# Strassen's form for one more step of the last batch pair, its transposes moved off TensorE, one input loaded earlier and one later, with a new order of work

## The chip, the cores and the metric

The kernel runs on one core of one Trainium2 chip. The metric is the device time of one execution in microseconds (us), taken as the median of several runs. A core has engines that each run their own instruction stream in order and meet through semaphores: TensorE (PE) with its matmuls and weight loads, VectorE (DVE), ScalarE (ACT), GpSimd (POOL), and SyncE (SP), which here issues most of the DMA transfers. PE writes its sums to PSUM banks, from which VectorE and ScalarE read them.

## The reference

Sixteen batches of 1024 nodes with 128 features go through two graph layers that share one symmetric 0/1 matrix `adj` (1024 x 1024). Cut to what is computed:

```python
# layer 0: attention over adj
h = x @ others_weight
u1, u2 = h @ a1, h @ a2
e = u1[:, idx1] + u2[:, idx2]            # pair indices: gathers from u1 and u2
e = jnp.where(e >= 0, e, ALPHA * e)
att = softmax(jnp.where(adj > 0, e, NEG_BIG), axis=1)
x = layernorm(x + att @ h + x @ self_weight)

# layer 1: five gated steps, in_matrix = out_matrix = adj
for step in range(5):
    m = adj @ h                          # m_in = m_out
    av = concat([m, m])
    u3 = h @ u3_w.T + u3_b
    z = sigmoid(av @ w3_w.T + w3_b + u3)
    r = sigmoid(av @ w4_w.T + w4_b + u3)
    hv = tanh(av @ w5_w.T + w5_b + (r * h) @ u5_w.T + u5_b)
    h = (1 - z) * h + z * hv
x = layernorm(x + h)
```

## The kernel before

**Pairs, steps and halves.** The batches run in eight pairs, q = 0 to 7, pair q holding batches 2q and 2q+1. For each pair there are layer 0 of its two batches and then the steps s = 0 to 4 of layer 1. Within a batch, h is kept transposed (features on the 128 partitions, nodes along the free side) in the tile hT and worked on in two halves of 512 nodes. The odd batch is kept with its sign flipped, and the signs of the activations are turned to fit.

**One step.** `messages` makes m = adj @ h. Its left operand are blocks of h with nodes on the partitions, each split by `split` into a high part (ACT cast, L661) and the rest (VectorE subtraction, L665), so that two fast matmuls carry the accuracy of one float32 matmul; `product` (L669 to L673) is eight such matmuls of 128x128 by 128x512. There are two forms. The plain form (pairs and steps in `PLAIN`) makes four products for each batch: 8 for the pair. The other is Strassen's, in Winograd's variant: the two batches side by side are cut into 2x2 blocks, and 7 products are made of the blocks x11, x12, x22 and of sums s1 to s4 that VectorE adds up first (`add_to`, L1127), with tables of adj's blocks as the right operand. ACT copies the results out (L1185, L1187) and VectorE combines them (L1195); the plain form has four ACT copies (L1158).

`gates` (from L1269) then makes, for each batch and half: the u3 product (L1301), a copy of it by ACT into the bank of the z gate (gz, L1304), the matmuls of r and z onto them (L1311), the tanh of each (L1314), r times h (L1321), the two matmuls of v (L1327, L1328), tanh (L1336), and three VectorE operations that give the new h (L1339, L1342, L1345).

**Turning h for the next step.** The blocks need nodes on the partitions, hT has features there. There are two ways. On PE (pairs and steps in `TURNED`, also some outputs; `on_pe`, L316): four 128x128 transposes for each half (`transposes`, L617 to L623), from which `split` reads in PSUM. Otherwise: VectorE transposes within 32x32 squares (`turn`, L631, tile T), `away` writes the squares to DRAM at swapped places with four 64 KB DMAs from SP (L641, X), and `back` reads 256 KB back (L649, tile G). The next step's splits and sums read G.

**Layer 0.** For each batch: x is loaded as xt (L703, L706), h and the two scores come from PE (L715), the scores are turned and sent to DRAM as ud (L760); pb reads one row of them back on all partitions (L767) and uu gathers 4-byte elements (L775). VectorE sums with adj and pb (junk, L854), and q (L843) and rz (L873 to L877) give the scales by which ACT (L906) and VectorE (L912) make the blocks blk for the products po (L673). For batches 4 to 7 the product of x with self_weight is made far ahead, in the first 40 us (`ahead`, from L474): x goes into tiles of the r and z pools (named r_x and z_x), the result (m_px) to DRAM as PX (L491), and it comes back when the batch's turn is there. For batch 7 that load waits until batch 1's gather uu is issued, as do the later weights (L383) and the xt loads of batches from 4 on.

**The order of work.** Every operation is given to a list scheduler, `Plan`, with its engine, an estimated length and a rank. A rank is 10 for each pair, 4.2 for each step, an offset for the kind of operation (the table `D`) and a correction for single batches, steps and halves (the table `NUDGE`). The scheduler plays the run through with these lengths and at each point lets an engine start the ready operation of lowest rank. What it finds is the order of each engine's instructions; on the chip each engine goes through its list in order. So a changed rank or length anywhere can move instructions elsewhere.

After all batches but the last ones are far, a flag that tells whether an exact second path is needed is read by every engine (L1789; the flag is written by VectorE, L1576); for SP this read stands in the middle of its stream of DMA issues.

Of the kernel before, what the change touches and what calls it, by code (L numbers as in the profile page):

```python
# [17 lines left out]
P = 128  # L18
N = 1024
HALF = 512  # L20
# [7 lines left out]
MOST = math.exp(HIGH - SHIFT)  # L28
TINY = 1e-30
LARGE = 0.999e30  # L30
PLAIN = {(0, 0), (0, 1), (0, 2), (7, 2), (7, 3), (7, 4)}
LATER = 0.75
AHEAD = range(4, 8)
LATE = 3001
TURNED = {(0, 0), (7, 2), (7, 3)}
IDLE = 44
NUDGE = {(3, 2): 1.8, (3, 3): 1.55, (0, 1): 0.15, (1, 1): 1.05, (2, 3): -1.05, (3, 1): -1.35, (3, 0): -0.15, (0, 2): 1.0, (2, 2): 1.25, (1, 4): 0.6, (1, 3): -2.85, (0, 3): -0.15, (1, 2): -0.15, (4, 0): 0.55, (2, 0): 2.25, (2, 1): 0.05, (4, 4): -1.7, (2, 4): 0.3, (7, 3): 1.1, (5, 4): -2.25, (4, 3): 0.8, (6, 3): 0.45, (6, 4): -0.05, (8, 2): 1.35, 10: 0.05, (11, 3): -0.9, (11, 4): 1.55, (7, 2): 1.0, (8, 3): -1.15, (12, 3): -0.45, (13, 3): 0.0, (12, 0): 1.6, (10, 3): -0.35, (8, 4): -0.55, (12, 4): -1.45, (12, 1): -0.95, (11, 2): -1.05, 12: 0.35, (13, 4): 2.7, (13, 0): 1.35, (11, 1): 1.1, (12, 2): -2.15, (10, 4): -1.1, (15, 0): -0.6, (14, 2): -0.6, (1, 0): -1.3, 3: -0.05, (0, 0): -0.3, (0, 4): 0.9, 4: -1.35, (4, 2): 0.05, (5, 1): -4.25, (3, 4): -0.25, 7: 0.75, (5, 3): 1.5, (6, 1): -0.25, (8, 1): 0.0, (9, 3): -4.85, 8: -1.65, (9, 2): -0.5, 11: 0.15, (7, 4): 1.2, 14: 0.1, (9, 1): 2.35, (15, 1): -0.5, (10, 2): 1.15, (14, 0): -0.45, (14, 3): 1.3, (11, 0): -0.2, (15, 4): 1.15, (15, 3): 1.2, 0: 0.85, (4, 1): -0.15, 6: -1.05, (7, 0): 0.35, (6, 2): -0.8, (5, 2): -0.6, (8, 0): 0.35, (6, 0): -0.05, (14, 4): -0.2, (14, 1): 0.3, 2: -0.35, (5, 0): 0.6, (7, 1): -0.35, (9, 0): -0.4, (9, 4): 0.9, 9: -0.15, (10, 0): 1.15, (10, 1): 0.0, 13: 0.15, (13, 2): -0.3, (15, 4, 0): 0.3, (15, 2): 0.3, ('add', 14, 1): 0.15, ('add', 15, 0): -0.1, ('ln', 14, 1): -0.5, ('ln', 15, 0): -1.2, 15: -0.05, ('add', 14, 0): -0.6, 1: 0.6, 5: 0.05, (13, 1): 0.15, ('ln', 15, 1): -0.05, ('old', 15): -0.05, ('add', 15, 1): 0.3}


class Plan:  # L40
# [106 lines left out]
def kernel(  # L147
# [51 lines left out]
    nc = tc.nc  # L199
# [27 lines left out]
    def exact(pools):  # L227
# [7 lines left out]
        tab = table.tile([P, 4, NC // 2, HALF], F32R, tag="tab", name="tab")  # L235
# [40 lines left out]
        def T(t, dtype=None, shape=None):  # L276
            if t not in tiles:
                _, sh, dt, _ = kinds[t[0]]
                tiles[t] = places[t[0]].tile(
                    shape or sh, dtype or dt, tag=t[0], name="_".join(map(str, t)).replace("-", "n")  # L280
                )
            return tiles[t]
# [25 lines left out]
        def sp(*a, **k):  # L308
            plan.add("SP", *a, **k)


        D = dict(m=0.45, pu=-0.1, u=3.45, pr=0.75, pz=0.85, r=1.45, pv=0.25, z=2.8, hv=0.5, h=-0.8, tr=1.85, o=6.35, ln=2.5, out=4.4, l1=-10.7, l2=-9, l3=-2.4, l4=-3.5, l5=-7.25)
        D.update(l6=-1.35, l7=-0.5, l8=-4.4, q=10, s=4.2, even=1, base=-1.0, q1=-3, b1=4.3, lz=-4.5, l1_0=-5.5, l2_0=-4, lz_0=-4.2, l3_0=-2, l4_0=-4.5, l5_0=-9, l6_0=-2.5, l7_0=-5, l8_0=-3.5)
        D.update(l1_1=-12, l2_1=-8, lz_1=-3, l3_1=-2.2, l4_1=-5, l5_1=-9.5, l6_1=-2.3, l7_1=-1.8, l8_1=-2, tab=8, tabc=1.5, cl=-5.4, ca=-50.5, cr=-51, px=-4.0, own=-2, ownw=-3.4)

        def on_pe(b, what):  # L316

# [33 lines left out]
        def early_loads():  # L351
# [14 lines left out]
            writes=[(boot, "early"), (ws, "early"), (x0, "early"), (("xt", 1), "early"), *((t, "early") for t in staged)],  # L366
# [13 lines left out]
        def late_loads():  # L380

            def load(t, what, to, by):
                sp(450, -7.9, lambda: nc.sync.dma_start(to(), by), reads=[(("b1",), 0)], writes=[(t, what)], lag=2600)  # L383

            for j, w in enumerate((w3_t, w4_t, w5_t)):
                load(
                    boot,
                    ("late", j),
                    lambda j=j: W("w345")[:, 256 * j : 256 * (j + 1)].rearrange("p (t e) -> p t e", t=2),
                    w.rearrange("(t p) e -> p t e", p=P),  # L390
                )
            load(("uw",), 0, lambda: u3, u3_t)
            load(("uw",), 1, lambda: u5, u5_t)
            for j, v in enumerate((w3_b, w4_b, w5_b, u3_b, u5_b)):
                load(ws, ("b", j), lambda j=j: T(ws)[j : j + 1, 3 * P : 4 * P], v.rearrange("(o p) -> o p", o=1))
# [78 lines left out]
        def ahead():  # L474
            for b in AHEAD:
                d = ("PX", b)
                for e in range(2):
                    bank, px, x = ("ps", "ahead", b, e), ("m", "px", b, e), ("rz"[e], "x", b)
                    hs = slice(e * HALF, (e + 1) * HALF)
                    sp(450, -91, lambda x=x, b=b, hs=hs: nc.sync.dma_start(T(x), x_t[b][:, hs]), reads=[(("b1",), 0)] if b == AHEAD[-1] else [], writes=[(x, "sent")], lag=0)  # L480
                    plan.add("DMA", 4 * 190, -102.7, lambda: None, reads=[(x, "sent")], writes=[(x, 0)])

                    def px_(bank=bank, x=x):
                        nc.tensor.matmul(T(bank), wsi, T(x), start=True, stop=True)

                    pe(F, 8000, px_, reads=[(x, 0), (("wsi",), 0)], writes=[(bank, 0)])
                    act(A, D["px"], lambda bank=bank, px=px: nc.scalar.copy(T(px), T(bank)), reads=[(bank, 0)], writes=[(px, 0)])
                    sp(
                        450,
                        -20,  # L490
                        lambda d=d, px=px, hs=hs: nc.sync.dma_start(T(d)[:, hs], T(px)),  # L491
                        reads=[(px, 0)],
                        writes=[(d, e)],
                    )
# [188 lines left out]
        def layer0(b):  # L683

            first = rank0(b) - (60 if b == 0 else 0)

            def lv(k):
                return D.get(f"{k}_{b}", D[k])

            rank = first + lv("l1")  # L690
            xt, hx, pb, u, us, uu, ud = (
                ("xt", b), ("hx", b), ("pb", b), ("u3", b), ("us", b), ("uu", b), ("ud", b)
            )
# [3 lines left out]
            if b in (2, 3):  # L697
                xt = ("hT", "x", b)
            junk = ("junk", b)
            q, zs, rz, hT = ("q", b), ("zs", b), ("rz", b), ("hT", b)  # L700
            yT, y0, yd = ([(k, b, g) for g in range(2)] for k in ("yT", "y0", "yd"))
            if b in (2, 3):
                sp(450, -90, lambda: nc.sync.dma_start(T(xt), x_t[b]), writes=[(xt, "sent")], lag=0)  # L703
                plan.add("DMA", 8 * 190, -102.5, lambda: None, reads=[(xt, "sent")], writes=[(xt, 0), (xt, 1)])
            elif b >= 2:
                sp(450, rank, lambda: nc.sync.dma_start(T(xt), x_t[b]), reads=[(("b1",), 0)], writes=[(xt, 0), (xt, 1)], lag=3500)  # L706

            for g in range(4):
                ph = ("ps", "g", b, "ph", g)
# [38 lines left out]
            if b >= 1:  # L748
# [5 lines left out]
                    reads=[(u, 0), (u, 1)],  # L754
                    writes=[(us, 0)],
# [5 lines left out]
                    reads=[(us, 0)],  # L761
                    writes=[(ud, 0)],
# [5 lines left out]
                    reads=[(ud, 0)],  # L768
                    writes=[(pb, 0), (pb, 1)],
                    lag=3000,  # L770
# [3 lines left out]
                    for w in range(2):  # L774
                        nc.sync.dma_start(T(uu)[:, w, :], T(ud)[w + 1].rearrange("(c p two) -> two p c", p=P, two=2)[w])  # L775

                sp(950, rank, uu_, reads=[(ud, 0)], writes=[(uu, 0), *([(("b1",), 0)] if b == 1 else [])], lag=3000)

            else:

                if True:

                    for e in range(2):
                        pp = ("ps", "p", b, e)
                        hs = slice(e * HALF, (e + 1) * HALF)
# [42 lines left out]
            rank = first + lv("l2")  # L828
# [21 lines left out]
            rank = rank0(b) + lv("lz")  # L850
# [17 lines left out]
            for k in range(2 if b == 0 else 1):  # L868
# [10 lines left out]
                def least_():  # L879
# [9 lines left out]
                    reads=[(q, 0), *((zs, c) for c in ks), *((("A",), c, 1) for c in ks)],  # L889
                    writes=[(rz, k)] if b == 0 else [(rz, 0), (rz, 1)],  # L890
# [5 lines left out]
            rank = rank0(b) + lv("l3")  # L896
            size = 1 if b == 0 else 4
            hl = [[("blk", b, w, g) for g in range(2)] for w in range(2)]
            for w in range(2):
                for c0 in range(0, NC, size):  # L900
# [20 lines left out]
                    r = [*((hx, g) for g in sorted({c // 2 for c in cs})), (rz, c0 // 4)]  # L921
# [3 lines left out]
            rank = rank0(b) + lv("l4")  # L925
            left = slice(0, HALF)
            right = slice(HALF, N)
            for g in range(2):
# [6 lines left out]
                for c0 in range(0, 4, size):  # L935
                    cs = range(c0, c0 + size)

                    def po_(g=g, po=po, cs=cs):
# [6 lines left out]
                        reads=[(k, 4 * g + c, j) for k, j in ((hl[0][g], 0), (hl[0][g], 1), (("A",), 0)) for c in cs],  # L945
                        writes=[(po, 0)],
# [7 lines left out]
            px = ("xt", b, "px") if b in AHEAD else ("gz", b, "px") if b == 0 else ("ps", "acc", b, "px")  # L954
            if b in AHEAD:
# [5 lines left out]
                    reads=[(d, 0), (d, 1), (hx, 3)],  # L961
                    writes=[(px, 0)],
                    lag=2800,
                )
            else:
# [4 lines left out]
                    reads=[(xt, 0), (("wsi",), 0), *([(yT[1], "p")] if b else [])],  # L970
                    writes=[(px, 0)],
# [5 lines left out]
                reads=[(px, 0), (yT[0], "s")],  # L977
                writes=[(yT[0], 0)],
# [61 lines left out]
            for g in range(2):  # L1040
# [5 lines left out]
                def h(g=g):  # L1046
# [9 lines left out]
                    lag=4000,  # L1056
# [783 lines left out]
```

## Time and profile before

| | us |
|---|---|
| median of 3 runs (1446.03 to 1447.8) | 1446.27 |
| the profiled execution's own time | 1445.98 |
| its span | 1444.2 |
| PE busy | 1429.6 (99%) |
| VectorE busy | 1158.9 (80%) |
| ScalarE busy | 891.8 (62%) |
| GpSimd busy | 198.0 (14%) |

The profile is of one execution of the program. The span runs from the first to the last instruction; the execution's own time is 1.8 us more. A busy time is the sum of the instructions of an engine. The chain that ended last is found from the last instruction back, at each step to what released it, so its shares say which engine set the end. A wait is given as engine, line and tile that waited, what released it, the total, the number of times and the longest. In the views by group or in time a row reads: line, engine, operation, out <- in, shapes, and in brackets the idle time just before and what ended it. The granted clock of TensorE was 0.998 of full speed on the mean.

### The profile page before, as it was taken

To read this page: it belongs to the slowest core of one execution; us is meant where nothing else is said; L and a number is where in the kernel's file an instruction comes from. 1 tells how busy PE (TensorE), PEld (TensorE's weight loads), DVE (VectorE), ACT (ScalarE), POOL (GpSimd) and SP (SyncE) were. 2 spreads that over 40 slices of the span, in tenths; PEclk is the share of its full clock that TensorE was granted. 3 is DMA by queue.
4 is the path that set the end of the run, shared out by engine and by line. 5 is a ranking of instruction groups with operands and counts; after the bars stand their busy time and mean duration, and the time that the engine had idled before them with its cause. 6 is when DMAs were issued, how large, how long until landed. Compare 5 with 4: busy or idle time off the path is not lost.

```text
span 1444.2 us, 17589 instructions
## 1 busy us (share of the span) xinstructions
PE 1429.6 (99%) x4955; PEld 897.0 (62%) x4955; DVE 1158.9 (80%) x2756; ACT 891.8 (62%) x1789; POOL 198.0 (14%) x324
## 2 busy tenths in 40 slices
PE   9999999999999999999999999999999999999997
PEld 7676666566666666566666665565656665556664
DVE  6897987998888988689888898677889876775635
ACT  5665665756666666567576667666666565654544
POOL 1121001003001021011110112010300212000202
PEclk9999999999999999999999999999999999999999
DMA  8334445534455544264444634444333544323111
GB/s 277 114 116 137 145 134 158 154 108 144 112 139 164 152 136 135 52 183 125 139 127 115 172 106 137 126 131 119 92 97 104 144 148 109 83 57 96 38 42 32
DMA packets 193458, 176.84 MB, mean 122 GB/s; under 512 B 37442, under 2 KB 142152, under 8 KB 193352
## 3 DMA queue, kind: packets, MB, share of 16 engines
q1 hardware_dynamic: 187046, 157.41, 39.2%
q0 software_dynamic: 5888, 17.83, 3.8%
q8 instruction: 41, 0.67, 0.2%
q14 instruction: 65, 0.53, 0.1%
q10 hardware_dynamic: 418, 0.39, 0.1%
HBM read 97.19 MB, written 78.36 MB: 122 GB/s over the span
## 4 chain that ended last, share of the span: by engine, by line
PE 97%; DVE 1%; DMA 1%; ACT 1%; issue 0%; SPq 0%; POOL 0%; POOLq 0%; DVEq 0%; ACTq 0%
PE ps_acc_a L673 17%; PE ps_g_r L1311 10%; PE gz L1311 9%; PE ps_g_v L1327 9%; PE ps_g_v L1328 9%; PE ps_g_r L1301 9%; PE ps_acc_c L673 9%; PE ps_acc_po L673 8%; PE ps_acc L673 6%; PE gz L673 4%; PE ps_g_ph L715 2%; PE ps_acc_po L983 1%; PE ps_acc_px L969 1%; PE ps_idle L449 1%; PE ps_t L623 1%; DMA uu<-ud 1%
## 5 line engine op out<-in xcount | busy, mean ns | idle before, releaser
L1339 DVE TENSOR_TENSOR hv<-hv,hT 128x512 f32<-128x512 f32 x158 | 108.4, 686 | 85.4 <-ACT hv L1336 84.4
L1327 PE MATMUL ps_g_v<-m,wm 128*128 128x512 f32 x318 | 162.6, 592 | 0.6 <-ACT m L1187 0.6
L1311 PE MATMUL ps_g_r<-m,wm 128*128 128x512 f32 x320 | 161.7, 593 | 0.7 <-ACT gz L1304 0.7
L1328 PE MATMUL ps_g_v<-r,u5h 128*128 128x512 f32 x318 | 162.4, 592 | 0.0
L1311 PE MATMUL gz<-m,wm 128*128 128x512 f32 x320 | 161.0, 592 | 0.0
L673 PE MATMUL ps_acc_a<-tab,blk_s 128*128 128x512 f32 x544 | 159.5, 435 | 0.0
L1301 PE MATMUL ps_g_r<-hT,u 128*128 128x512 f32 x320 | 158.9, 592 | 0.0
L1321 DVE SCALAR_TENSOR_TENSOR r<-r,hT 128x512 f32<-128x512 f32 x160 | 109.2, 684 | 60.5 <-ACT r L1314 60.1
L1314 ACT ACTIVATE r<-ps_g_r,bh 128x512 f32<-128x512 f32 x160 | 109.9, 687 | 68.2 <-PE ps_g_r L1311 67.9
L673 PE MATMUL ps_acc_po<-adj,blk 128*128 128x512 f32 x512 | 144.8, 427 | 2.4 <-DVE blk L912 1.4
L673 PEld LDWEIGHTS ps_acc_a<-tab,blk_s 128*128 128x128 f32 x544 | 102.4, 188 | 45.5 <-issue 23.7
L1304 ACT COPY gz<-ps_g_r 128x512 f32<-128x512 f32 x160 | 91.2, 575 | 50.8 <-PE ps_g_r L1301 49.8
L673 PEld LDWEIGHTS ps_acc_po<-adj,blk 128*128 128x128 f32 x512 | 95.7, 188 | 40.6 <-issue 15.6
L1314 ACT ACTIVATE z<-gz,bh 128x512 f32<-128x512 f32 x160 | 109.1, 688 | 18.5 <-PE gz L1311 18.2
L1342 DVE SCALAR_TENSOR_TENSOR hv<-z,hv 128x512 f32<-128x512 f32 x159 | 108.0, 682 | 3.7 <-ACT z L1314 2.2
L1345 DVE SCALAR_TENSOR_TENSOR hT<-hv,hT 128x512 f32<-128x512 f32 x158 | 107.2, 682 | 1.4
L1328 PEld LDWEIGHTS ps_g_v<-r,u5h 128*128 128x128 f32 x318 | 60.2, 189 | 76.2 <-issue 60.4
L1311 PEld LDWEIGHTS gz<-m,wm 128*128 128x128 f32 x320 | 60.6, 190 | 73.4 <-issue 72.8
L673 PE MATMUL ps_acc<-adj,blk_h 128*128 128x512 f32 x384 | 104.0, 419 | 0.0
L631 DVE STREAM_TRANSPOSE T<-hT 128x512 f32<-128x512 f32 x142 | 99.0, 701 | 0.9 <-issue 0.3
L1336 ACT ACTIVATE hv<-ps_g_v,nb 128x512 f32<-128x512 f32 x80 | 54.9, 686 | 71.5 <-PE ps_g_v L1328 71.2
L665 DVE TENSOR_TENSOR blk_s<-G,blk_s 128x512 fp32r<-128x512 f32 x136 | 91.5, 680 | 4.8 <-ACT blk_s L661 4.5
(211 smaller groups left out, 2522.6 us busy)
## 6 DMA issues: line engine op xcount, KB each, us to landing
G<-X SPq DMA_DIRECT2D x144, 256.0 KB
X<-T SPq DMA_DIRECT2D x568, 64.0 KB
yd<-y POOLq DMA_DIRECT2D x32, 256.0 KB, 3.0
D_y<-T_y SPq DMA_DIRECT2D x112, 64.0 KB
F_y<-D_y SPq DMA_DIRECT2D x28, 256.0 KB
X<-y SPq DMA_DIRECT2D x28, 256.0 KB
D_b<-T_b SPq DMA_DIRECT2D x112, 64.0 KB
F_b<-D_b SPq DMA_DIRECT2D x28, 256.0 KB
```

What stands on the lines that cost most here:

```text
L631: nc.vector.transpose(T(t).rearrange("p (b c i) -> p b c i", b=4, c=4), turned(src()))
L665: lambda: nc.vector.tensor_tensor(half(1), src(), half(0), ALU.subtract),
L673: nc.tensor.matmul(T(bank), T(blk)[:, k, c, :], right(c), start=(first and i == 0), stop=(last and i == len(terms) - 1), skip_group_check= ...
L1301: nc.tensor.matmul(T(pr), u3, h(), start=True, stop=True)
L1311: nc.tensor.matmul(T(p_), wm[:, j, :], T(m), start=False, stop=True, skip_group_check=True)
L1314: nc.scalar.activation(T(t), T(p_), AF.Tanh, bias=bh[:, j : j + 1], scale=0.5 * sg)
L1321: lambda r=r, h=h: nc.vector.scalar_tensor_tensor(T(r), T(r), 1.0, h(), ALU.add, ALU.mult),
L1327: nc.tensor.matmul(T(pv), wm[:, 2, :], T(m), start=True, stop=False)
L1328: nc.tensor.matmul(T(pv), u5h, T(r), start=False, stop=True)
L1339: nc.vector.tensor_tensor(T(hv), T(hv), h(), ALU.subtract)
L1342: nc.vector.scalar_tensor_tensor(T(hv), T(z), 1.0, T(hv), ALU.add, ALU.mult)
L1345: nc.vector.scalar_tensor_tensor(h(), T(hv), 0.5, h(), ALU.mult, ALU.add)
```

## The change

Five things change.

1. (7, 2) leaves `PLAIN`: step 2 of the last pair (batches 14 and 15), the third of its five steps, is made in Strassen's form. Steps 3 and 4 of that pair stay plain.
2. (7, 2) and (7, 3) leave `TURNED`: h after steps 2 and 3 of the last pair is turned by VectorE and DRAM, not by PE. Since step 1's output has gone that way before, step 2 reads from G in either form.
3. The early x of batch 7 goes into two tiles of pool "o" (the pool of the late residuals) and no longer waits for an event; before, it went into tiles of the r and z pools after batch 1's gather.
4. The xt loads of batches from 4 on wait for batch 2's gather uu, not batch 1's. The late weights still wait for batch 1's; only the name of the event is new.
5. `NUDGE` and `D` are set anew: some 66 entries of `NUDGE` differ or are added, and in `D` among others u (the gz copy) 3.45 to 4.15, pz 0.85 to 0.65, hv 0.5 to -1.5, h -0.8 to -2.8.

```diff
-PLAIN = {(0, 0), (0, 1), (0, 2), (7, 2), (7, 3), (7, 4)}
+PLAIN = {(0, 0), (0, 1), (0, 2), (7, 3), (7, 4)}
...
-TURNED = {(0, 0), (7, 2), (7, 3)}
+TURNED = {(0, 0)}
...
-        D = dict(m=0.45, pu=-0.1, u=3.45, pr=0.75, pz=0.85, r=1.45, pv=0.25, z=2.8, hv=0.5, h=-0.8, tr=1.85, o=6.35, ln=2.5, out=4.4, l1=-10.7, l2=-9, l3=-2.4, l4=-3.5, l5=-7.25)
+        D = dict(m=0.45, pu=-0.1, u=4.15, pr=0.75, pz=0.65, r=1.45, pv=0.25, z=2.8, hv=-1.5, h=-2.8, tr=1.85, o=6.35, ln=2.5, out=4.4, l1=-10.5, l2=-8, l3=-4.4, l4=-3.5, l5=-7.25)
...
-                sp(450, -7.9, lambda: nc.sync.dma_start(to(), by), reads=[(("b1",), 0)], writes=[(t, what)], lag=2600)
+                sp(450, -7.9, lambda: nc.sync.dma_start(to(), by), reads=[(("b", 1), 0)], writes=[(t, what)], lag=2600)
...
-                    bank, px, x = ("ps", "ahead", b, e), ("m", "px", b, e), ("rz"[e], "x", b)
+                    bank, px = ("ps", "ahead", b, e), ("m", "px", b, e)
+                    x = ("o", "x", b, e) if b == AHEAD[-1] else ("rz"[e], "x", b)
                     hs = slice(e * HALF, (e + 1) * HALF)
-                    sp(450, -91, lambda x=x, b=b, hs=hs: nc.sync.dma_start(T(x), x_t[b][:, hs]), reads=[(("b1",), 0)] if b == AHEAD[-1] else [], writes=[(x, "sent")], lag=0)
+                    sp(450, -91, lambda x=x, b=b, hs=hs: nc.sync.dma_start(T(x, shape=[P, HALF]), x_t[b][:, hs]), writes=[(x, "sent")], lag=0)
...
-                sp(450, rank, lambda: nc.sync.dma_start(T(xt), x_t[b]), reads=[(("b1",), 0)], writes=[(xt, 0), (xt, 1)], lag=3500)
+                sp(450, rank, lambda: nc.sync.dma_start(T(xt), x_t[b]), reads=[(("b", 2), 0)], writes=[(xt, 0), (xt, 1)], lag=3500)
...
-                sp(950, rank, uu_, reads=[(ud, 0)], writes=[(uu, 0), *([(("b1",), 0)] if b == 1 else [])], lag=3000)
+                sp(950, rank, uu_, reads=[(ud, 0)], writes=[(uu, 0), *([(("b", b), 0)] if b in (1, 2) else [])], lag=3000)
```

In the changed file the lines from about 478 on have a number higher by one than those named here.

More of the change, by code (lines that the diff above doesn't have):

```diff
@@ L34 @@
 LATE = 3001
-TURNED = {(0, 0), (7, 2), (7, 3)}
+TURNED = {(0, 0)}
 IDLE = 44
-NUDGE = {(3, 2): 1.8, (3, 3): 1.55, (0, 1): 0.15, (1, 1): 1.05, (2, 3): -1.05, (3, 1): -1.35, (3, 0): -0.15, (0, 2): 1.0, (2, 2): 1.25, (1, 4): 0.6, (1, 3): -2.85, (0, 3): -0.15, (1, 2): -0.15, (4, 0): 0.55, (2, 0): 2.25, (2, 1): 0.05, (4, 4): -1.7, (2, 4): 0.3, (7, 3): 1.1, (5, 4): -2.25, (4, 3): 0.8, (6, 3): 0.45, (6, 4): -0.05, (8, 2): 1.35, 10: 0.05, (11, 3): -0.9, (11, 4): 1.55, (7, 2): 1.0, (8, 3): -1.15, (12, 3): -0.45, (13, 3): 0.0, (12, 0): 1.6, (10, 3): -0.35, (8, 4): -0.55, (12, 4): -1.45, (12, 1): -0.95, (11, 2): -1.05, 12: 0.35, (13, 4): 2.7, (13, 0): 1.35, (11, 1): 1.1, (12, 2): -2.15, (10, 4): -1.1, (15, 0): -0.6, (14, 2): -0.6, (1, 0): -1.3, 3: -0.05, (0, 0): -0.3, (0, 4): 0.9, 4: -1.35, (4, 2): 0.05, (5, 1): -4.25, (3, 4): -0.25, 7: 0.75, (5, 3): 1.5, (6, 1): -0.25, (8, 1): 0.0, (9, 3): -4.85, 8: -1.65, (9, 2): -0.5, 11: 0.15, (7, 4): 1.2, 14: 0.1, (9, 1): 2.35, (15, 1): -0.5, (10, 2): 1.15, (14, 0): -0.45, (14, 3): 1.3, (11, 0): -0.2, (15, 4): 1.15, (15, 3): 1.2, 0: 0.85, (4, 1): -0.15, 6: -1.05, (7, 0): 0.35, (6, 2): -0.8, (5, 2): -0.6, (8, 0): 0.35, (6, 0): -0.05, (14, 4): -0.2, (14, 1): 0.3, 2: -0.35, (5, 0): 0.6, (7, 1): -0.35, (9, 0): -0.4, (9, 4): 0.9, 9: -0.15, (10, 0): 1.15, (10, 1): 0.0, 13: 0.15, (13, 2): -0.3, (15, 4, 0): 0.3, (15, 2): 0.3, ('add', 14, 1): 0.15, ('add', 15, 0): -0.1, ('ln', 14, 1): -0.5, ('ln', 15, 0): -1.2, 15: -0.05, ('add', 14, 0): -0.6, 1: 0.6, 5: 0.05, (13, 1): 0.15, ('ln', 15, 1): -0.05, ('old', 15): -0.05, ('add', 15, 1): 0.3}
@@ new lines @@
+NUDGE = {(3, 2): 1.95, (3, 3): 0.35, (0, 1): 0.15, (1, 1): 1.05, (2, 3): -1.05, (3, 1): -1.35, (3, 0): -0.15, (0, 2): 1.0, (2, 2): 1.25, (1, 4): 0.0, (1, 3): -2.85, (0, 3): -0.15, (1, 2): -0.1, (4, 0): 0.55, (2, 0): 2.3, (2, 1): -0.25, (4, 4): -1.7, (2, 4): 0.25, (7, 3): 1.4, (5, 4): -2.85, (4, 3): 0.5, (6, 3): 1.05, (6, 4): 1.15, (8, 2): 1.35, 10: 0.05, (11, 3): -2.1, (11, 4): 1.85, (7, 2): 0.4, (8, 3): -1.0, (12, 3): 0.75, (13, 3): 0.9, (12, 0): 1.65, (10, 3): -0.35, (8, 4): -0.85, (12, 4): -1.45, (12, 1): -0.95, (11, 2): -2.3, 12: 0.35, (13, 4): 1.7, (13, 0): 1.35, (11, 1): 1.1, (12, 2): -2.15, (10, 4): -1.7, (15, 0): -0.3, (14, 2): -1.5, (1, 0): -1.3, 3: -0.05, (0, 0): -0.3, (0, 4): 0.95, 4: -1.35, (4, 2): -0.1, (5, 1): -3.65, (3, 4): -0.3, 7: 1.05, (5, 3): 1.5, (6, 1): -0.4, (8, 1): 0.0, (9, 3): -5.45, 8: -1.05, (9, 2): -0.65, 11: 0.3, (7, 4): 2.35, 14: 0.1, (9, 1): 2.35, (15, 1): -1.75, (10, 2): 1.75, (14, 0): -0.45, (14, 3): 0.65, (11, 0): -0.2, (15, 4): 1.15, (15, 3): 0.7, 0: 0.85, (4, 1): 1.05, 6: -0.9, (7, 0): 0.3, (6, 2): -2.3, (5, 2): 0.0, (8, 0): 0.7, (6, 0): 0.55, (14, 4): -0.2, (14, 1): 0.3, 2: -0.35, (5, 0): 0.6, (7, 1): -0.35, (9, 0): -0.55, (9, 4): 0.8, 9: -0.1, (10, 0): 1.15, (10, 1): -0.6, 13: 0.15, (13, 2): -0.9, (15, 4, 0): 0.25, (15, 2): 1.65, ('add', 14, 1): 0.2, ('add', 15, 0): -0.15, ('ln', 14, 1): -1.7, ('ln', 15, 0): -1.2, 15: -0.05, ('add', 14, 0): -0.7, 1: 0.6, 5: 0.1, (13, 1): -0.45, ('ln', 15, 1): -0.05, ('old', 15): 0.55, ('add', 15, 1): 0.3, ('ln', 14, 0): 0.05, ('first', 15): 1.05, (14, 4, 1): -0.15, (14, 4, 0): 1.2, (15, 4, 1): 1.2}
@@ L309, in sp @@
             plan.add("SP", *a, **k)
-        D = dict(m=0.45, pu=-0.1, u=3.45, pr=0.75, pz=0.85, r=1.45, pv=0.25, z=2.8, hv=0.5, h=-0.8, tr=1.85, o=6.35, ln=2.5, out=4.4, l1=-10.7, l2=-9, l3=-2.4, l4=-3.5, l5=-7.25)
-        D.update(l6=-1.35, l7=-0.5, l8=-4.4, q=10, s=4.2, even=1, base=-1.0, q1=-3, b1=4.3, lz=-4.5, l1_0=-5.5, l2_0=-4, lz_0=-4.2, l3_0=-2, l4_0=-4.5, l5_0=-9, l6_0=-2.5, l7_0=-5, l8_0=-3.5)
-        D.update(l1_1=-12, l2_1=-8, lz_1=-3, l3_1=-2.2, l4_1=-5, l5_1=-9.5, l6_1=-2.3, l7_1=-1.8, l8_1=-2, tab=8, tabc=1.5, cl=-5.4, ca=-50.5, cr=-51, px=-4.0, own=-2, ownw=-3.4)
+        D = dict(m=0.45, pu=-0.1, u=4.15, pr=0.75, pz=0.65, r=1.45, pv=0.25, z=2.8, hv=-1.5, h=-2.8, tr=1.85, o=6.35, ln=2.5, out=4.4, l1=-10.5, l2=-8, l3=-4.4, l4=-3.5, l5=-7.25)
+        D.update(l6=-1.35, l7=-0.5, l8=-3.9, q=10, s=4.2, even=1, base=-1.0, q1=-3, b1=4.3, lz=-4.5, l1_0=-5.5, l2_0=-4, lz_0=-4.2, l3_0=-2, l4_0=-4.5, l5_0=-9, l6_0=-4.5, l7_0=-5.5, l8_0=-3.5)
+        D.update(l1_1=-12, l2_1=-10, lz_1=-3, l3_1=-2.2, l4_1=-5, l5_1=-9.5, l6_1=-1.3, l7_1=0.2, l8_1=-2, tab=8.5, tabc=1.5, cl=-5.4, ca=-49.5, cr=-52.8, px=-4.0, own=-3, ownw=-3.4)
         def on_pe(b, what):
```

## The prediction

> **What bounds the kernel now.** I read the page first, then the chain that ended last.
>
> ```profile
> PE 1429.6 (99%) x4955; PEld 897.0 (62%) x4955; DVE 1158.9 (80%) x2756; ACT 891.8 (62%) x1789; POOL 198.0 (14%) x324
> PE 97%; DVE 1%; DMA 1%; ACT 1%; issue 0%; SPq 0%; POOL 0%; POOLq 0%; DVEq 0%; ACTq 0%
> ```
>
> TensorE (PE) is busy in 99% of the span and is 97% of the chain. VectorE's 80% and ScalarE's 62% are beside it. So a matmul taken away shortens the run by its own length unless its operands then come late, and the rest to win is the few places where PE waits. The waits of PE over the whole span, largest first:
>
> ```profile
> PE gz_fill L453 <- POOL ident masks.py:199: 1.4, 1, 1.4
> PE ps_acc_po L673 <- DVE blk L912: 1.4, 1, 1.4
> PE ps_acc_po L673 <- ACT blk L906: 1.0, 1, 1.0
> PE ps_g_r L1311 <- ACT gz L1304: 0.7, 1, 0.7
> PE ps_g_v L1327 <- ACT m L1187: 0.6, 1, 0.6
> ```
>
> The first is the start. The next two are one place, layer 0 of batch 1 at 53 us; the fourth lies at 1250 us. What is behind the 53 us place shows in three views: VectorE's waits from 30 to 62 us, its timeline, and SyncE's (SP's) queue.
>
> ```profile
> DVE junk L854 <- DMA pb<-ud: 4.1, 1, 4.1
> ```
>
> ```profile
> 39.38 0.53 SPq L760 DMA_DIRECT2D ud<-us  x1
> 39.97 0.49 SPq L706 DMA_DIRECT2D xt<-in_x_dram  x1
> 40.55 0.85 SPq L491 DMA_DIRECT2D PX<-m_px  x2
> 41.50 0.44 SPq L767 DMA_DIRECT2D pb<-ud  x1
> 41.99 2.28 SPq L775 DMA_DIRECT2D uu<-ud  x2
> ```
>
> ```profile
> 50.57 0.16 DVE L834 TENSOR_TENSOR seen<-uu 128x4 f32<-128x4 f32 x1 [0.29 <-DMA uu<-ud]
> 51.86 0.16 DVE L873 TENSOR_TENSOR rz<-cnt,q 128x8 f32<-128x8 f32 x1
> 54.60 1.14 DVE L912 SCALAR_TENSOR_TENSOR blk<-hx,rz,blk 128x128 fp32r<-128x128 f32 x4
> ```
>
> Batch 1's scales (rz L873) stand on VectorE behind batch 2's row copy pb and gather uu, which land at 49.6 and 50.5. The first needed blk of batch 1 comes 4.1 us after uu, and PE waits twice, 2.4 us, 2.9 with the slow first matmul.
>
> For the 1250 us place, SP's waits from 1235 to 1252 us and ScalarE's (ACT's) timeline:
>
> ```profile
> SPq L1789 <- DVE flag L1576: 4.5, 1, 4.5
> ```
>
> ```profile
> 1248.81 0.62 ACT L661 CAST blk_x<-G 128x512 fp32r<-128x512 f32 x1 [2.41 <-DMA G<-X]
> 1249.34 1.06 ACT L1304 COPY gz<-ps_g_r 128x512 f32<-128x512 f32 x2
> ```
>
> SP stood 4.5 us at the read of the flag, so G was fetched late, the cast held ACT, the gz copy behind it came late, and PE lost 0.97 us there (idle plus a slower first matmul; 0.7 named as wait).
>
> For the end of the run, the table of stretches (columns: PE, PE loads, VectorE, ACT, POOL busy; clock; DMA share; GB/s):
>
> ```profile
> 1340.00:1380.00 40.00, 40.00 (x150) 25.70 (x148) 18.93 (x46) 20.39 (x38) 9.51 (x15) 1.00 0.14 43
> 1380.00:1420.00 40.00, 40.00 (x137) 23.98 (x136) 16.64 (x25) 18.04 (x29) 0.00 (x0) 1.00 0.04 15
> ```
>
> and two steps of its chain, the prices of what goes:
>
> ```profile
> 1359.40 0.44 PE ps_t L623 x4
> ...
> 1367.86 1.87 PE ps_acc L673 x8
> ```
>
> **The change part by part.** *Work taken off PE.* Step 2 of the last pair (batches 14 and 15) is done with 7 products in place of 8: 1.87 us less. Steps 2 and 3 of both batches no longer turn h on PE: 2 steps x 2 batches x 2 halves = 8 groups of four transposes, 8 x 0.435 = 3.48. PE is the bound in that stretch (40.00 of 40.00 us), so all of it counts: **-5.35**.
>
> *What takes its place.* Strassen's form adds 4 adds, 3 splits and 2 combines on VectorE, the turn 8 transposes: 17 x 0.68-0.70 = 11.7 us; on ACT 3 casts (0.616) and a copy (0.58), 2.4 us; on SP 32 stores (1.77 for four) and 8 loads (about 0.4), 17 us of issue; 4 MB of DMA. The stretch has VectorE at 47 and 42%, ACT at 51 and 45%, DMA at 14 and 4%, and SP issues next to nothing, so as work it costs **0**. As a chain it must fit: in the pair's previous turn, v is done at 1305.9, ACT's tanh ends at 1306.8, three VectorE steps and the turn end at 1309.7, the store's issue begins at 1309.75, the load's 3.3 us later, the cast 3.4 us after that (1316.50), and the low half could be there at 1317.8: 11.9 us from v to both halves. Between v and the first product that needs it, the new order leaves PE work of 14.2 to 16.5 us at seven of the eight half-turns of plain steps and more at the others (at the Strassen step 19.8 and up; one of 23). So the nearest has some 2 us to spare; by hand, with what else stands on ACT and VectorE, about 1. I take 0; if the cover is gone, a half-turn costs what it exceeds 14.2 by (rival 3). In the new order the u product, its gz copy and the z gate of 15's step 3, second half, lie directly behind each other: PE waits for drain, 0.53-0.57 of copy and wake-up, **+0.8**. Three others (14's steps 3 and 4, 15's step 4, first halves) have one matmul pair, 0.86, in between; a like case waited 0.07 before: **+0.45** in all (0.2 to 0.8). At the end the layer norm of the last batch follows v with one group of statistics put first: **+0.2** (-0.3 to +0.4); the 5.5 us from the last scale to the span's end stay.
>
> *Batch 7's x loaded early, batch 4's late.* Two SP issues (0.82 us) leave the queue between 33 and 39 us and go to the first 15 us, where 0.5 MB more takes 1.35 us of DMA at 380 KB/us; PE first needs what stands behind it at 31.8 us and DMA drained at 23, so 0. With them and a shorter row of weights ahead, ud of batch 2, whose source is written at 37.1, can go at 37.5 in place of 39.4, pb at about 39.6 in place of 41.5; the 512 KB of xt (1.35 us) now stand behind uu instead of before pb. But uu itself still stands behind batch 7's two stores, which wait for ACT until 40.8, so it can be issued only some 0.5 us earlier and gains by the emptier queue. Batch 1's uu, issued at 27.1, was taken by 32.7 on a queue as full: 5.6 us; on 41.4 that gives 47, against 50.5. My bounds are 46.5 and 50. At 47 the lo half of blk is ready near 51.5, and PE comes there at about 51.8. So the 2.9 us go. Against this, the new VectorE order puts the bias and weight sums ahead of the low half of batch 0's first block: it is ready 0.6 to 0.9 us later, and PE's wait of 0.47 at 42 us grows to about 1.05. Net **-2.0** (bounds +0.5, uu as late as before, to -2.9). The wait that xt of batch 4 gets is met by the queue's order alone, since it stands right behind uu; what queues behind it are more xt loads, and its first reader on PE comes after 65 us: 0.
>
> *The flag.* In the new order SP reads the flag behind a store that itself needs VectorE past the flag's copy, so nothing is queued behind a wait: **-0.97** (0, if something else holds that cast, to -1.0).
>
> *Ranks anew.* Other waits of PE (0.45 at 247 us, 0.4 to 0.6 at 1201) may go or come back elsewhere. The whole known stall outside start and end is 5 us in 1400, so I take **0**; bounds -0.9 (both gone) and, upward, a few waits of the size of the 1250 us one.
>
> Sum: -5.35 + 0.8 + 0.45 + 0.2 - 2.0 - 0.97 = -6.9 on the profiled execution's 1445.98 (span 1444.2, 1.8 around it): 1439.1. That execution lies 0.3 below the median of 1446.27, so **1439.4**.
>
> **The rivals.** (1) The early wait stays: uu decides, and it stands behind the same stores. For it: the issue moves by half a microsecond only. Against: 512 KB less ahead. Time 1439.4 + 2.0 = 1441.4, or 1441.9 with the upper bound.
>
> (2) New waits from the new order. The ranks of some 66 entries move, and every one can put an ACT or VectorE step in front of one that PE needs, as the cast stood before gz at 1249. Three to six such waits of 0.97 give +3 to +6: 1442.4 to 1445.4. For it: VectorE is 80% busy. Against: PE's waits between 60 and 1420 us add up to under 3 us under the old ranks.
>
> (3) The other side: the chain through DRAM is not covered. Place: the eight half-turns of the last pair, where PE-turned blocks needed no DMA. Price: each exposes what its chain is above 14.2 us. A gain of 6.9 is turned into a loss of 2.9 from (6.9 + 2.9)/8 = 1.2 us each, a chain of 15.4. For it: a transfer can be much slower than the 3.4 us here; pb took 8.1 us from 41.50 to its first use at 49.58. [...] Against: pb had the DMA engines full, here they are at 4 to 14%. [...]
>
> (4) Better than the sum: the small new waits don't show, and 247 and 1201 us go too: 1439.4 - 1.25 - 0.9 = 1437.2 or below.
>
> **How the numbers follow.** No change that this kernel's runs can tell is about 0.2%, 2.9 us: bounds 1443.4 and 1449.2. The sum within 2 us (1437.4 to 1441.4) 0.55; rival 1 (to 1442.4) 0.13; rival 2 0.14, of it 0.04 below 1443.4, 0.09 inside and 0.01 above; rival 3 0.08, 0.07 of it above 1449.2; rival 4 0.10. Faster: 0.55 + 0.13 + 0.04 + 0.10 = 0.82; same 0.10; slower 0.08. The range 1436 to 1444.5 leaves out about 0.03 below and 0.12 above.
>
> **What would show it.** Transposes at L623 fall from 100 records to 68, matmuls at L673 by 8; PE's wait for blk at 53 us gone and VectorE's wait for pb well under 4.1; no SP wait at the flag; a new wait of z's gate for gz (0.6 to 0.8) in the last 60 us, and no wait of ps_acc for blk there. Wrong if PE waits there for a cast or a split fed by G, or if PE's stalls between 60 and 1420 us exceed 6 us.

## The result and the profile after

The changed kernel takes 1439.65 us (median of 6 runs, 1438.91 to 1440.42) against 1447.39 for the kernel before (6 runs). The ratio is 0.9948, 95% interval 0.9935 to 0.9961: 7.5 us faster. The profiled execution is the slowest of the six, 1440.42 us with a span of 1438.6, so the two traces show only 5.6 us of it: in the trace of after, PE lost some 0.45 us more in the first 20 us than in that of before, and runs of one kernel differ by 1.5 to 2.2 us.

The head of the page after, the shares of the chain, and PE's waits over the whole span:

```profile
PE 1423.9 (99%) x4915; PEld 891.1 (62%) x4915; DVE 1172.8 (82%) x2773; ACT 895.2 (62%) x1793; POOL 195.9 (14%) x324
...
PE 98%; DVE 1%; DMA 1%; ACT 0%; POOL 0%; SPq 0%; issue 0%; DVEq 0%; ACTq 0%; POOLq 0%
```

```profile
PE gz_fill L453 <- POOL ident masks.py:199: 1.4, 1, 1.4
PE ps_acc L674 <- DVE blk_h L666: 0.9, 1, 0.9
PE ps_acc_c L674 <- ACT r L1315: 0.8, 1, 0.8
PE gz L1312 <- ACT gz L1305: 0.7, 1, 0.7
PE gz L1312 <- ACT m L1188: 0.2, 1, 0.2
```

PE has 40 records less, 32 transposes and 8 matmuls, and 5.7 us less of busy time. VectorE has 14 us more and ACT 3.4, and the chain does not see them. The two waits for blk at 53 us are gone, so is the one of the r gate at 1250 us. Three others stand out in the list now: the wait for the low half of batch 0's first block, at 43.8 us, has grown, and those at 207 us and at 1386 us are new.

VectorE's waits from 30 to 62 us, SP's queue and VectorE's timeline in the place where the scales of batch 1 came late:

```profile
DVE seen L835 <- DMA uu<-ud: 0.7, 1, 0.7
```

```profile
37.59 0.53 SPq L761 DMA_DIRECT2D ud<-us  x1
38.23 0.99 SPq L492 DMA_DIRECT2D PX<-m_px  x2
39.60 0.32 SPq L768 DMA_DIRECT2D pb<-ud  x1
40.75 0.80 SPq L492 DMA_DIRECT2D PX<-m_px  x2
41.61 1.61 SPq L776 DMA_DIRECT2D uu<-ud  x2
```

```profile
46.91 0.16 DVE L835 TENSOR_TENSOR seen<-uu 128x4 f32<-128x4 f32 x1 [0.73 <-DMA uu<-ud]
...
48.20 0.16 DVE L874 TENSOR_TENSOR rz<-cnt,q 128x8 f32<-128x8 f32 x1
...
50.95 1.14 DVE L913 SCALAR_TENSOR_TENSOR blk<-hx,rz,blk 128x128 fp32r<-128x128 f32 x4
```

ud goes at 37.6 and pb at 39.6 us; uu is issued only 0.4 us earlier than before, but taken 3.7 us earlier. The block is begun at 50.95 and PE comes to it at 52.0.

PE's timeline at the two places where it waits anew, and the stretches of the last pair:

```profile
42.39 0.48 PE L674 MATMUL ps_acc<-adj,blk_h 128*128 128x512 f32 x1
43.80 1.91 PE L674 MATMUL ps_acc<-adj,blk_h 128*128 128x512 f32 x7 [0.93 <-DVE blk_h L666]
```

```profile
1384.50 1.02 PE L1302 MATMUL ps_g_r<-hT,u 128*128 128x512 f32 x2
1386.23 1.12 PE L1312 MATMUL gz<-m,wm 128*128 128x512 f32 x2 [0.71 <-ACT gz L1305]
```

```profile
1340.00:1380.00 40.00, 40.00 (x125) 22.58 (x125) 26.18 (x54) 26.71 (x50) 8.13 (x12) 1.00 0.32 90
1380.00:1420.00 40.00, 39.28 (x131) 23.46 (x131) 20.01 (x45) 17.68 (x29) 3.17 (x7) 1.00 0.27 78
```

In the second, the z gate stands directly behind its own u product. In the third, VectorE went from 47 and 42% to 65 and 50%, DMA from 14 and 4% to 32 and 27%, and PE stays full but for that one wait. No product of the last pair waits for a block.

### The profile page after: what moved, and what is told of

The parts are those of the page before. It is cut to its first block, busy times and chain, and to the rows that moved or that the text cites. A ratio compares the mean times of both kernels' runs of the same rounds, so it can differ in the third digit from the quotient of the medians.

```text
span 1438.6 us, 17605 instructions
## 1 busy us (share of the span) xinstructions
PE 1423.9 (99%) x4915; PEld 891.1 (62%) x4915; DVE 1172.8 (82%) x2773; ACT 895.2 (62%) x1793; POOL 195.9 (14%) x324
## 3 DMA queue, kind: packets, MB, share of 16 engines
q1 hardware_dynamic: 192806, 161.61, 39.6%
## 4 chain that ended last, share of the span: by engine, by line
PE 98%; DVE 1%; DMA 1%; ACT 0%; POOL 0%; SPq 0%; issue 0%; DVEq 0%; ACTq 0%; POOLq 0%
PE ps_acc_a L674 18%; PE gz L1312 10%; PE ps_g_r L1312 9%; PE ps_g_v L1328 9%; PE ps_g_v L1329 9%; PE ps_g_r L1302 9%; PE ps_acc_c L674 9%; PE ps_acc_po L674 8%; PE ps_acc L674 5%; PE gz L674 4%; PE ps_g_ph L716 2%; PE ps_acc_po L984 1%; PE ps_idle L449 1%; PE ps_acc_px L970 1%; PE ps_ahead L485 0%; DMA G<-X 0%
## 5 line engine op out<-in xcount | busy, mean ns | idle before, releaser
L674 PE MATMUL ps_acc_a<-tab,blk_s 128*128 128x512 f32 x560 | 162.8, 432 | 0.0
L632 DVE STREAM_TRANSPOSE T<-hT 128x512 f32<-128x512 f32 x150 | 105.0, 704 | 3.2 <-DMA D_y<-T_y 2.3
L1312 PEld LDWEIGHTS ps_g_r<-m,wm 128*128 128x128 f32 x320 | 60.3, 189 | 73.8 <-issue 73.4
L1128 DVE TENSOR_TENSOR G<-G,G 128x512 f32<-128x512 f32 x140 | 95.4, 682 | 0.8
```

Of the source, the lines that this page charges most:

```text
L632: nc.vector.transpose(T(t).rearrange("p (b c i) -> p b c i", b=4, c=4), turned(src()))
L674: nc.tensor.matmul(T(bank), T(blk)[:, k, c, :], right(c), start=(first and i == 0), stop=(last and i == len(terms) - 1), skip_group_check= ...
L1128: lambda: nc.vector.tensor_tensor(T(t), T(t), T(other), ALU.add),
L1312: nc.tensor.matmul(T(p_), wm[:, j, :], T(m), start=False, stop=True, skip_group_check=True)
```

## The experiments

Four kernels keep the scheduler and change parts of the inputs to it. Two put more copies into one transfer and keep the order of work. The others keep a finished order and move single operations in it, with this edit, in which a pair (i, j) puts operation i ahead of operation j:

```diff
-            for i in plan.order():
+            steps = plan.order()
+            for i, j in MOVES:
+                steps.remove(i)
+                steps.insert(steps.index(j), i)
+            for i in steps:
                 plan.ops[i][3]()
```

Below, "PE's lost time" is the time between PE's instructions that is more than the instructions' own pace: the start of each instruction in the trace less the summed work ahead of it. It is 12.7 us in the trace of before and 10.7 in that of after, of it 6.4 and 6.8 in the first 20 us; the work itself is 1422.6 and 1417.2 us.

**The parts alone.** Strassen's form alone, on the kernel before:

```diff
-PLAIN = {(0, 0), (0, 1), (0, 2), (7, 2), (7, 3), (7, 4)}
+PLAIN = {(0, 0), (0, 1), (0, 2), (7, 3), (7, 4)}
```

> The kernel before with (7, 2) alone taken out of PLAIN; ranks, loads and PE's transposes as before. Theory (a product less is its length less, 1.87 us, since PE is the bound and step 2's blocks came through DRAM before too): 1.9 us below the kernel before, transposes still 100 records, no PE wait over 0.5 us in the last 150 us. Rival (the gain of the change is the new order; Strassen's sums come too late under the old ranks): 0 to 3 us above it, with PE waits for blk_s or blk_x of the last pair.

Measured: ratio 0.9987 (0.9977 to 0.9997), 1.9 us faster. PE's work fell by 1.87 us and the list of its waits is that of before.

The transposes alone, on the kernel before:

```diff
-TURNED = {(0, 0), (7, 2), (7, 3)}
+TURNED = {(0, 0)}
```

> The kernel before with (7, 2) and (7, 3) taken out of TURNED and nothing else. Theory: eight groups of four transposes less, 3.5 us below the kernel before, if the old ranks leave 14 us of PE work in each half-turn; what is not covered shows as PE waits for blk_h from a G of steps 3 and 4 and is taken off the 3.5. Rival (the chain through DRAM is exposed): waits of 1.2 us and more at most of the eight half-turns, so 6 us above the kernel before or worse.

Measured: ratio 0.9991 (0.9981 to 1.0001), 1.3 us faster, not told from nothing and short of the 3.5 expected. PE's work fell by 3.48 us, and 1.9 us of it came back at one place. PE's waits from 1370 to 1385 us of this kernel, and ACT's timeline just ahead of it:

```profile
PE ps_acc L673 <- ACT blk_h L661: 1.1, 1, 1.1
PE ps_acc L673 <- DVE blk_h L665: 0.3, 1, 0.3
```

```profile
1375.94 1.64 ACT L569 ACTIVATE o<-o,rstd_o 128x128 f32<-128x128 f32 x4
1377.48 0.60 ACT L661 CAST blk_h<-G 128x512 fp32r<-128x512 f32 x1
```

The cast had to stand behind four scalings of a layer norm: its G was there. So it is the place in ACT's order that was late, not DMA.

Both together, on the kernel before:

> The kernel before with both sets changed, old ranks and old loads. Theory: PE's work falls by 5.35 us; the waits at 53 us (2.9) and 1250 us (1.0) stay in kind, so 5.4 us below the kernel before less what the old ranks expose. Rival (the new order carries the gain): no more than 2 us below.

Measured: ratio 1.0046 (1.0028 to 1.0064), 6.7 us slower. The expectation missed by 12 us. PE's work did fall by the 5.35 us. But the scheduler, with the old ranks, now put the last two steps' products close behind each other; PE's waits from 1390 to 1410 us, its timeline, and the stretch from 1400 to 1407 us, whose last three figures are granted clock, DMA share and GB/s:

```profile
PE ps_acc L673 <- ACT blk_h L661: 3.1, 1, 3.1
PE ps_acc L673 <- DVE blk_h L665: 1.1, 1, 1.1
```

```profile
1400.61 0.79 PE L673 MATMUL ps_acc<-adj,blk_h 128*128 128x512 f32 x1 [3.14 <-ACT blk_h L661]
1402.55 7.67 PE L673 MATMUL ps_acc<-adj,blk_h 128*128 128x512 f32 x23 [1.15 <-DVE blk_h L665]
```

```profile
1400.00:1407.00 7.00, 5.25 (x12) 3.78 (x13) 3.02 (x5) 1.17 (x2) 0.00 (x0) 0.52 0.59 158
```

ACT's timeline shows what the two casts of that place waited for:

```profile
1399.94 0.62 ACT L661 CAST blk_h<-G 128x512 fp32r<-128x512 f32 x1 [1.75 <-DMA G<-X]
1401.24 0.62 ACT L661 CAST blk_h<-G 128x512 fp32r<-128x512 f32 x1 [0.69 <-DMA G<-X]
```

Here the chain through DRAM is exposed, as rival 3 had it: 4.3 us of waiting in a row, and then 23 matmuls in 7.67 us where 23 x 0.233 is 5.4, since the granted clock was 0.52 for these 7 us. 7.1 us are lost in that one place, 3.4 more from 1350 to 1375 us. The early place lost 2 us more than before as well: its two waits were 0.4 us longer, and the matmuls behind them ran slow (granted clock 0.68 from 54 to 58 us, where the kernel before has 1.00).

New ranks and loads with the old forms:

```diff
-PLAIN = {(0, 0), (0, 1), (0, 2), (7, 3), (7, 4)}
+PLAIN = {(0, 0), (0, 1), (0, 2), (7, 2), (7, 3), (7, 4)}
-TURNED = {(0, 0)}
+TURNED = {(0, 0), (7, 2), (7, 3)}
```

> The changed kernel with the two sets put back, so new ranks and new loads with the old forms. Theory: 5.35 us of PE work come back, 5 us above the changed kernel, 2.5 us below the kernel before; the wait at 53 us stays gone. Rival (the order carries the gain): within 1.5 us of the changed kernel.

Measured: ratio 0.9973 (0.9963 to 0.9983), 3.9 us faster than before, some 3.6 slower than the changed kernel; expected were 2.5 and 5. PE's work is 1422.6 again and its lost time 8.1 us. So new order and loads are worth 3.9 us with the old forms, and the forms are worth 3.6 us with the new order, but -6.7 with the old one. The parts do not add up: the order pays for the forms.

**How much cover the new order leaves.** The changed kernel, with G of the last pair's steps 3 and 4 read by way of one more copy in DRAM, and in another run of two:

```diff
-                back(x, t, rank, [(t, "place")])
+                if (q, s) in ((7, 3), (7, 4)):
+                    def by_way():
+                        last = T(x)[:, 0:HALF]
+                        for n in range(1):
+                            y = T(("Y", b, s, g, n))
+                            nc.sync.dma_start(y, last)
+                            last = y
+                        nc.sync.dma_start(T(t), last)
+                    sp(450, rank, by_way, reads=[(x, 0), (t, "place")], writes=[(t, 0)], lag=LATE)
+                else:
+                    back(x, t, rank, [(t, "place")])
```

> The changed kernel in the same order on every engine, but G of the last pair's steps 3 and 4 is read by way of a copy from DRAM to DRAM (one DMA more in each of the eight half-turns, waited for by SP). Theory (the chain is 12 us and has 1 to 3 us to spare at the nearest half-turn, 14.2 to 16.5 us of cover): one hop of about 3 us more goes 0.5 to 2 us past the cover at most of the eight, so 3 to 8 us above the changed kernel. Rival A (the chain was much shorter than 12 us or the cover wider, so DRAM plays no part): within 1 us of it. Rival B (the chain already set PE's pace there): 8 x 3 = 24 us above it.

> As the run with one hop more, with two. Theory: the second hop has no cover left and counts in full where half-turns follow each other: 8 to 16 us above the run with one. Rival A: no more than 3 us above it.

Measured: with one hop 1.0023 (1.0013 to 1.0033) of the kernel before, which is 10.8 us above the changed kernel (0.9948); with two, one run of 1467.86 us, 17 above that. The direction is that of the theory and both rivals of the run with one hop fall, but both times lie above the expected ranges (3 to 8 and 8 to 16). It is not the length of the hop: in the trace it takes 2.9 to 3.4 us from its own issue to that of the load, about the 3 us assumed. PE's lost time says more. PE's waits from 1400 to 1412 us of the run with one hop, and ACT's timeline there:

```profile
PE gz L1325 <- ACT gz L1318: 3.7, 1, 3.7
```

```profile
1408.35 0.62 ACT L663 CAST blk_h<-G 128x512 fp32r<-128x512 f32 x1 [4.54 <-DMA G<-Y]
1408.88 0.58 ACT L1318 COPY gz<-ps_g_r 128x512 f32<-128x512 f32 x1
```

The largest loss, 5.6 us with the slow matmuls behind it, is not at a product that reads the late block. It is at a z gate, whose copy stands on ACT behind a cast that waits 4.5 us for DMA. In the last pair PE loses some 10 us more than in the trace of after, 6.5 of it behind two such gates and 3.6 at products. SP's queue adds to the hop: SP stands from 1402.5 to 1405.6 us until one copy has landed, so the T of the next half-turn, ready at 1402.3, is stored only from 1406.0.

In the trace of after the low halves of the four blocks of step 4 are ready 1.8 to 2.7 us before PE starts on them, and those of step 3 1.2 to 3.9 us.

**The early place.** On the kernel before, in its own order, batch 4's xt load alone moved behind uu (MOVES = [(442, 511)]: that load ahead of the next xt load):

> The kernel before in its own order, but the xt load of batch 4 stands behind batch 2's gather uu on SP's queue; nothing else moves. Theory (512 KB ahead of uu cost it 1.35 us, its issue 0.5): uu taken 1.3 to 2 us earlier than 50.5 us, PE's wait at 53 to 55 us falls from 2.9 to 1.0 to 1.6 us, time 1.3 to 2 us below the kernel before. Rival (uu is late by its own place behind batch 7's stores or by ud): uu within 0.5 us of 50.5, no change.

Measured: ratio 0.9973 (0.9964 to 0.9983), 3.9 us faster, more than the 1.3 to 2 expected. VectorE's waits from 30 to 62 us:

```profile
DVE junk L854 <- DMA pb<-ud: 1.5, 1, 1.5
```

uu is taken at 47.2 us in this trace, whose start is 0.8 us ahead of that of before, so 2.6 us earlier. PE's loss at 52 us is 0.3 in place of 2.9; the trace shows no place for the rest of the 3.9. It is as much as the new order and loads together gave with the old forms: there the flag's 1.0 us was won as well, and about as much was lost again in the longer wait at 43.8 us and the new one at 207 us.

The other way round, on the changed kernel, that load put back ahead of pb and uu (MOVES = [(442, 169)]: ahead of the first store to PX behind ud):

> The changed kernel in its own order, but batch 4's xt load stands right behind ud of batch 2 on SP, ahead of pb and uu, as it stood before the change; batch 7's x stays early. Theory (the 512 KB ahead decide, the other moves on SP do not): uu is taken 2 to 2.6 us later than 46.9, the first low half of blk 1 to 1.5 us after PE gets there, so 1 to 2.5 us above the changed kernel, with a PE wait for blk at 52 to 54 us. Rival (the earlier ud and the shorter queue are enough): no wait there, the time of the changed kernel.

Measured: ratio 0.9953 (0.9938 to 0.9968), not told from the changed kernel, and no PE wait from 46 to 60 us. uu is taken at 47.5 us, 1.2 us later against the trace's own start, and that was within the slack. So either is enough for the stall: the load moved back, or what else the changed kernel does there, the earlier ud and pb and the shorter queue among it; no run takes these apart. The theory that the 512 KB alone decide falls.

**The flag.** On the kernel before, in its own order, PE's sum and VectorE's copy of the flag some 10 us earlier (MOVES = [(5265, 4588), (5266, 4606)]: the sum, then the copy):

> The kernel before in its own order, but PE's sum for the flag and VectorE's copy of it stand some 10 us earlier, so that SP reads the flag before the batch 14 stores. Theory: SP's wait for the flag falls from 4.5 to under 1 us, the cast from G at 1248.8 comes before the u3 products, and PE's wait for gz at 1250 us (0.97 with the slow matmul) is gone: 1.0 us below the kernel before. Rival (the G load waits for its own store or turn, not for SP): the wait for gz stays.

Measured in one run: 1446.04 us against 1447.65, a time inside the spread of the kernel before (from 1445.64), so the trace has to decide. SP's wait for the flag is 1.8 us, not under 1, and there is no PE wait at 1250 us: PE's loss of 0.97 there is gone and its lost time is otherwise that of before. The chain from SP's read to the gate is shown by that.

**The new waits.** The changed kernel with six operations moved, which the two expectations count as seven (MOVES = [(275, 215), (276, 215), (1626, 1628), (5117, 5126), (5238, 5218), (5240, 5245)]; the first of them does not change an engine's order):

> The changed kernel with seven operations moved by hand in its finished order and nothing else: the cast and low half of batch 0's first block ahead of the bias and weight sums on VectorE; at 207 us the x12 product ahead of the s1 product; at 1386 us the v products of batch 15, step 3, first half ahead of the z gate of the second; in the tail the transposes of batch 15's first half one place forward on PE and their statistics ahead of the second half's on VectorE. Theory (each of these waits is one of order, and PE is the bound before and behind it): waits of 1.2, 1.06 and 0.98 us at 43.8, 207 and 1386 us fall by 0.9, 0.9 and 0.9, the tail by 1.1: 3.8 us below the changed kernel, 11.5 below the kernel before (0.9921). Rival (the waits move to the next instruction): within 1 us of the changed kernel.

Measured: ratio 0.9929 (0.9916 to 0.9943), 1437.33 us: some 2.7 us below the changed kernel. The intervals of the two ratios touch; the traces agree, with 8.1 us of PE's lost time against 10.7. The three waits are gone, the tail from the last v to the last scale is 8.9 us in place of 9.8, and 1.1 us came back in a new place. PE's waits from 1395 to 1401 us, and ACT's timeline:

```profile
PE gz L1312 <- ACT gz L1305: 1.0, 1, 1.0
```

```profile
1398.68 0.62 ACT L662 CAST blk_h<-G 128x512 fp32r<-128x512 f32 x1 [1.90 <-DMA G<-X]
1399.20 0.58 ACT L1305 COPY gz<-ps_g_r 128x512 f32<-128x512 f32 x1
```

It is the pattern of the runs with hops: PE came earlier, the G did not, and the gz copy stood behind its cast. So that copy was put ahead of the cast (in addition MOVES = [..., (5154, 5171), (5155, 5171)]):

> The run with seven operations moved, and on ACT the cast of batch 15's G (step 4, first half) now stands behind the gz copy of batch 14's second half instead of ahead of it; its low half goes along. Theory (the wait of 1.1 us at 1399.8 us is the copy queued behind a cast that waits for DMA): that wait is gone, the cast is 0.5 us later with some 1 us to spare, 1.0 us below the run before, 12 below the kernel before (0.9917). Rival (that stretch is paced by the DMA chain itself): the wait comes back at the product that reads the block, no gain.

Measured: ratio 0.9923 (0.9910 to 0.9937), 1435.59 us. PE has no wait left between 50 us and the last v. It has the lowest time of all versions, some 3.6 us below the changed kernel by the ratios; from the run before it the time does not tell it (the intervals overlap), the missing wait does.

## Why the prediction was right

The forecast was 1439.4 us, and 1439.65 came. That the two lie 0.25 us apart is luck in part: the forecast took 6.9 us off a median of 1446.27, the six runs of the kernel before have 1447.39, the gain by the ratio is 7.5 us and by the two traces 5.6. Several terms were also off and cancelled. Step by step, in the trace:

- *Work taken off PE, -5.35.* It is -5.35: PE's work went from 1422.6 to 1417.2, and the run with Strassen's form alone gave its 1.87 us as 1.9.
- *What takes its place, 0, with 14.2 us or more of cover against 11.9.* No product waits. The slack was 1.2 us at the nearest of the eight half-turns, as against about 1 taken by hand, and the last half-turn took 11.2 us from v to its low half. The 0 holds for the new order alone: under the old ranks the same forms lost 10.5 us of PE's time in the last pair. The prediction read the cover from the new order, and so this term already held what "Ranks anew" was worth to it.
- *The gates, +0.8 and +0.45.* The first is 0.98 us at 1386 us. The three others did not show: a term of 0.45 that measured 0.
- *The early loads, net -2.0.* uu was taken at 46.9 us, against 47 forecast. PE lost 2.9 us less at 53 us and 0.73 more at 43.8: -2.2. The reason was only half right. The prediction gave the 512 KB 1.35 us; the run that moved that load alone measured 2.6, and the one that put it back 1.2.
- *The flag, -0.97.* It is gone, and the run with the early flag shows that the flag was its cause.
- *Ranks anew, 0.* Small waits at 247, 1201 and 1235 us are gone (0.45, 0.43 and 0.2), and one of 1.06 us came at 207 us, at a product whose bank ACT's tanh still had to read. The 0 was a sum of two mechanisms, of which rival 2 named the kind of the one and rival 4 the other.
- *The tail, +0.2.* It is +0.7 from the last v to the last scale. The chain in the tail of after shows it:

```profile
1424.39 0.43 PE ps_g_v L1245 x2
1424.83 0.44 PE ps_t L1255 x4
1425.27 0.45 PE ps_t L1262 x4
1425.72 0.45 PE ps_t L1255 x4
1426.16 0.45 PE ps_t L624 x4
...
1426.64 0.69 DVE y_o L1397
```

The transposes of the first half (L624) stand behind three groups of the second's, 3.1 us after the last v (1423.10), where they stood 2.2 us after it (1429.72, 1431.93). The prediction counted the statistics put first, and not these groups.

Together, up to the last v: -5.35 - 2.2 - 0.97 - 1.1 + 1.06 + 0.98 + 0.45 (start) = -7.1 against 6.6 in the trace; the rest is waits of 0.1 to 0.3. Behind it 0.7 for the tail and 0.3 for the output's last transfers give the 5.6 us by which the spans differ.

Rival 1 did not come about (2.2 of 2.9 us net). Rival 3 did not either, but it is real: under the old ranks its mechanism made the same forms slower than before, and one hop more made the changed kernel slower than before, too. The prediction's price for it, what a chain exceeds 14.2 us by at each of eight half-turns, gives some 5 to 9 us in all for a chain of 11.9 us and a hop of 2.9 to 3.4 us; the run with one hop lies 10.8 us above the changed kernel. More than half of what PE lost there, 6.5 of some 10 us, was lost through ACT's queue and not at the products that read the blocks, a way that the prediction named for rival 2 and did not price in rival 3. The DMA share was 27 to 32% there after the change, and no product waited. What the chain takes when the engines are as full as pb had them (a share of 0.89 to 1.12 from 43 to 48 us of the kernel before) no run here shows.

## What to carry to other kernels

When work goes from the engine that sets the pace to a longer chain on others, the saving is certain and the cover is not: read the distance in the bounding engine's own order between the producer and the first use, in the order that will run, and compare it with the chain measured in a like place. Look in each in-order queue of that chain for what stands behind the operation that waits, since here a late transfer hurt the copy queued behind its cast more than its own reader (6.5 us of PE's time against 3.6 in the run with one hop), and a wait of 3.1 us on SP held back the next half-turn's stores (T ready at 1402.3 us, stored from 1406.0). When a stretch has no other bound, single waits of about 1 us can be taken out by moving one operation past one other, one after the other, until the next one shows (here those of 1.2, 1.06 and 0.98 us, until one of 1.1 showed).

## What the runs showed of the hardware that was not expected

- In these runs a wait of PE could cost more than itself. After 3.1 and 1.1 us with a single matmul between them, the granted clock was 0.52 from 1400 to 1407 us and 23 matmuls took 7.67 us in place of 5.4. After 3.7 us in the run with one hop it was 0.57 to 0.58 from 1410 to 1414 us, and the two matmuls of the r gate took 1.91 us in place of 1.02. After single waits of 0.7 to 1.1 us nothing of the kind showed: in the trace of after the granted clock was 1.00 in the stretches behind those of 0.9, 0.8 and 0.7 us (44 to 48, 207 to 211 and 1386 to 1390 us). The two waits of 1.0 and 1.4 us at 53 us cost 0.5 us beyond themselves in the kernel before, at a clock of 1.00 from 54 to 58 us; two waits of 1.4 us there in the run with both forms cost some 2 us beyond themselves, at a clock of 0.68. So the clock fell after waits of 3.1 and 1.1 us and after two of 1.4, and not after 1.0 and 1.4. Why like waits cost different amounts, no run here shows.
- One 512 KB load ahead of a 4-byte gather on SP's queue cost the gather 2.6 us in one order and 1.2 in another.
